# Attention's block border rewritten: projections, the whole weight sum and ScalarE's end-of-block work moved to one place, one addition for four heads

## The chip, the cores and the metric

The kernel runs on one core of one Trainium2 chip. The metric is the device time of one execution in microseconds; several runs of the same program are summarised by their median. A profiled execution gives, for every instruction, its start, its length and what it waited for. Four engines matter here: TensorE (PE, matmuls; its weight loads are listed as PEld), VectorE (DVE), ScalarE (ACT) and SyncE (SP, which issues transfers). Each takes its instructions strictly in the order of the program; between engines there are only semaphores.

## What is computed

The input is x of shape (16, 384, 16, 16) in float32. Four layers follow each other; only the first is touched by the change in what it computes with, the others by their order.

```python
def layer0(x, qk_w, alpha, beta, gamma):          # 2 batches x 2048 tokens, 12 heads of 32
    xt = tokens(x)                                # (2, 2048, 384)
    q, k = split(xt @ qk_w.T)                     # per head
    attn = softmax(q * 32**-0.5 @ k.T)            # (2, 12, 2048, 2048)
    attn = alpha * eye + beta * attn - gamma / 2048
    return attn @ xt_heads                        # v is x itself
```

Layer 1 is a ConvNeXt block (depthwise 7x7 convolution, layer norm, 384 to 1536, gelu, global response norm, 1536 to 384, residual), layer 2 a fusion block with depthwise 3x3 filters, a 768 to 384 matmul, norm and gelu, and layer 3 a linear-attention block with an MLP (384 to 1536 to 384). All of it is float32.

## The kernel before, in words

**Attention.** The function attention (L400) works through 6 units, one for each batch and group of four heads (128 channels). A unit has 4 blocks of 512 queries (NBLK), so there are 24 blocks, numbered 0 to 23. A block has 16 iterations (NQC), t = 0 to 15, one for each 128 keys. An iteration has these steps.

- scores (L465): four matmuls, one for each head, write st, two PSUM tiles of two heads each. Two ScalarE activations (exponential) turn them into e, 128 x 1024 each. Below, e(t) is the result of iteration t.
- weighted (L483): four matmuls add e times v into av. It is called one iteration late: PE gets st(t+1), then av(t).
- In weighted, too, VectorE adds e(t) to a running sum s, with two additions of 128 x 1024, one for each pair of heads. The tuple ADDS says after how many iterations a running sum is handed on: 16, 8 or 4 for each block.
- weights (L526): matmuls with a matrix of ones sum s over the keys and add it to dn, the softmax's denominator. In mid-block it is cut into four parts that are spread over later iterations; at the end of a block it is whole, four matmuls of 512 columns, two iterations after the block's last av.
- finish (L538) turns dn into a reciprocal and applies it: on ScalarE r (copy of dn), w (logarithm), w (exponential of the negative); on VectorE two refining steps r, then va times r, then the sum with xg. The steps are put one by one into the iterations 2 to 8 of the next block. va (copy of av) and xg are made by ScalarE right after the block's last av.
- project (L578): at iteration SLOT = 5 of a block, two steps of the projections: six matmuls p (three for each 128 x 512 result) and two ScalarE copies, into q of this unit or k of the next one. A step for k also issues the load of v on SP. Blocks 0 to 20 have two steps, block 21 has one, blocks 22 and 23 have none.

Three PSUM tiles of two banks (tag st) are shared by the scores and the projections; av and dn have a bank each. The e tiles last for four iterations.

**Order.** Everything goes through a recording layer (class InOrder, L98) which pins the instructions to the order in which the code emits them; that is why nearly all rows of the profile have the line L98. Work that is due later is kept in the dictionary due, by iteration. After each iteration, fill (L1505) puts work of layer 1 into VectorE's queue: mostly the depthwise 7x7 convolution (rows y<-l,vec,y; 48 multiply-add steps for each of 3 chunks of each of 8 blocks), and the first layer norms of two blocks. How much fits is reckoned by pace (L196) from assumed lengths: pe, the length of an iteration, less dve, VectorE's additions and finishing steps.

**Later work.** After attention a planner (class Plan, all at L182) orders the remaining tasks of layers 1 to 3 by assumed lengths, ranks (RANK) and a tolerance (SLACK).

Of the kernel before, what the change touches and what calls it, by code (L numbers as in the profile page):

```python
# [9 lines left out]
F32 = mybir.dt.float32  # L10
AF = mybir.ActivationFunctionType
ALU = mybir.AluOpType
# [3 lines left out]
P = 128  # L16
# [12 lines left out]
NBLK = N // BLK  # L29
NIP = NBLK  # L30
NQC = N // P
SLOT = 5
LEAD = 20 * NQC + 6
FIRST = NQC + 10

TURNS = (
    (0, ((0, 0), (0, 1), (0, 2), (0, 3),)),
# [6 lines left out]
AFTER = ('x4', 0, 2)  # L44

RANK = {
    "mid": ((7.3, 48.9, 70.4, 82.6), (148.1, 31.6, -5.4, 26.9)),
    "l1": ((125.5, 116.9, 31.6, 62.9), (92.4, 221.3, 38.4, 14.0)),
    "l3c": ((153.2, 335.5, -64.8, 29.8), (10.7, 30.4, 62.7, 79.9)),
    "conv": 470.9,  # L50
}
SLACK = 0.1944
LOGEXP = "natural_log_exp_and_others"
JUNK = 2

ADDS = (16, 16, 16, 16, 8, 16, 8, 4, 4, 16, 16, 16, 8, 8, 4, 8, 16, 16, 8, 8, 4, 8, 4, 4)
XB, YB, SB = 12, 4, 23
NLEAD = 2
TB = BLK // P
RB = 2 * HW  # L60
HD3 = 48
MOST, LEAST, TINY = 1e18, 1e-11, 1e-19
# [133 lines left out]
def pace(t):  # L196


    n, i = divmod(t - 1, NQC)
    adds = ADDS[n]  # L200
    pe, dve = 2.066, 2.275 if t and i % adds else 0.0
    at = i - adds - 1
    parts = sum(j * adds // 4 == at % adds for j in range(4)) if at >= 0 else 0
    if parts:
        pe += 0.22 * parts
    elif i == 1 and n > 0:
        pe += 0.87
    else:
        pe += 0.09
    if n > 0:  # L210
        dve += {5: 0.66, 6: 0.66, 7: 0.6, 8: 0.66}.get(i, 0.0)
    return pe, dve


# [185 lines left out]
def attention(tc, X, xt, L0, block, small, col, cols, ones, load_qk, banks, fill, bound, tiny):  # L400
# [6 lines left out]
    with ExitStack() as actx:  # L407
        pool = lambda name, bufs, **kw: actx.enter_context(tc.tile_pool(name=name, bufs=bufs, **kw))
        wqk_sb = pool("wqp", 1).tile([P, NC, 2, NC, P], F32, name="wqk_sb")
        load_qk(wqk_sb)  # L410
        ep = pool("ep", 8)
        sp = pool("sp", 4)
        op = pool("op", 2)
        pst = pool("pst", 3, space=PSUM)
        pacc = pool("pacc", 1, space=PSUM)
# [37 lines left out]
            return made, early, late  # L453


        due = {}

        def unit(u, made, gm):

            b, g = units[u]  # L460
            q, keys, v = made["q"], made["k"], made["v"]
            adds = ADDS[u * NBLK : (u + 1) * NBLK]
            acc, sums = {}, {}

            def scores(n, t):  # L465
                es = []
                for i in range(2):
                    es.append(ep.tile([P, 2, BLK], F32, tag="e", name=f"e_{u}_{n}_{t}_{i}"))
                sts = [bank2(f"st_{u}_{n}_{t}_{i}") for i in range(2)]
                for h in range(4):  # L470
                    rows = slice(HD * h, HD * (h + 1))
                    pe.matmul(
                        sts[h // 2][:, h % 2, :],
                        keys[t // TB][rows, ts(t % TB, P)],
                        q[n][rows, :],
                        start=True,
                        stop=True,
                    )
                for i in range(2):
                    act.activation(es[i], sts[i], AF.Exp, scale=HD**-0.5)  # L480
                return es

            def weighted(n, t, es):  # L483
                if t == 0:
                    acc["av"] = pacc.tile([P, BLK], F32, tag="av", name=f"av_{u}_{n}")
                for h in range(4):
                    pe.matmul(
                        acc["av"][HD * h : HD * (h + 1), :],
                        v[t // TB][:, (t % TB) * P + HD * h : (t % TB) * P + HD * (h + 1)],
                        es[h // 2][:, h % 2, :],  # L490
                        start=(t == 0),
                        stop=(t == NQC - 1),
                    )
                at = t % adds[n]
                for i in range(2):
                    if at == 0:
                        sums[i] = es[i]
                    elif at == 1:
                        s = sp.tile([P, 2, BLK], F32, tag="s", name=f"s_{u}_{n}_{t}_{i}")
                        dve.tensor_tensor(s, sums[i], es[i], ALU.add)  # L500
                        sums[i] = s
                    else:
                        dve.tensor_tensor(sums[i], sums[i], es[i], ALU.add)


                k = (u * NBLK + n) * NQC + t
                if at == adds[n] - 1:
                    parts = 1 if t == NQC - 1 else 4
                    for i in range(parts):
                        due.setdefault(k + 2 + i * adds[n] // 4, []).append(  # L510
                            lambda i=i, summed=dict(sums): weights(
                                n, t, summed, ts(i, BLK // parts)
                            )
                        )
                for f in due.pop(k, ()):
                    f()
                if t == NQC - 1:
                    va = op.tile([P, BLK], F32, tag="va", name=f"va_{u}_{n}")
                    act.activation(va, acc["av"], AF.Copy, scale=1.0)
                    xg = op.tile([P, BLK], F32, tag="xg", name=f"xg_{u}_{n}")  # L520
                    act.activation(
                        xg, X[b][n][:, g, :], AF.Identity, scale=col("alpha", g), bias=gm
                    )
                    due[k + 2].append(lambda: finish(n, va, xg))

            def weights(n, t, summed, at):  # L526
                if t == adds[n] - 1 and at.start == 0:
                    acc["dn"] = pacc.tile([P, BLK], F32, tag="dn", name=f"dn_{u}_{n}")
                for h in range(4):
                    pe.matmul(  # L530
                        acc["dn"][HD * h : HD * (h + 1), at],
                        ones[:, :HD],
                        summed[h // 2][:, h % 2, at],
                        start=(t == adds[n] - 1 and at.start == 0),
                        stop=(t == NQC - 1),
                    )

            def finish(n, va, xg):  # L538

                if g == 0:  # L540
                    L0[b][n] = block(f"l0_{b}_{n}")
                k = u * NBLK + n
                r = op.tile([P, BLK], F32, tag="r", name=f"r_{u}_{n}", bufs=1)
                w = op.tile([P, BLK], F32, tag="w", name=f"w_{u}_{n}", bufs=1)
                act.activation(r, acc["dn"], AF.Identity, accum_out=bound[:, 0, k : k + 1])

                def log():
                    act.activation(w, r, AF.Ln, bias=tiny)

                def invert():  # L550
# [12 lines left out]

                def put():
                    dve.scalar_tensor_tensor(
                        L0[b][n][:, g, :], va, col("beta", g), xg, ALU.mult, ALU.add
                    )

                for i, f in enumerate([log, invert, defect, refine, scale, put]):
                    due.setdefault((k + 1) * NQC + 3 + i, []).append(f)  # L570

            return scores, weighted

        means = [channel_means(dve, op, X, cols, b, act if b else None) for b in range(NB)]
        for b, (_, steps) in enumerate(means):
            for i, s in enumerate(steps):
                due[b * NC * NBLK * NQC - 36 * b + (3 - b) * i] = [s]
        def project(name, steps):  # L578
            pp = bank2(name)
            for copy in [f(pp[:, i, :]) for i, f in enumerate(steps)]:  # L580
                copy()
            return 2.7 * len(steps)

        made, early, late_steps = projections(*units[0])
        for i in range(0, len(early), 2):
# [4 lines left out]
        for u, (b, g) in enumerate(units):  # L590
# [5 lines left out]
            for n in range(NBLK):  # L596
                for t in range(NQC):
                    es = scores(n, t)
                    added = 0.0
                    if before:  # L600
                        before()
                    before = lambda f=weighted, a=(n, t, es): f(*a)
                    if t == SLOT and steps:
                        added = project(f"p_{u}_{n}", steps[:2])
                        del steps[:2]
                    fill((u * NBLK + n) * NQC + t, added)
            assert not steps
        before()
        while due:
            for f in due.pop(min(due)):  # L610
                f()
# [4 lines left out]
def conv_seq_kernel(  # L616
# [882 lines left out]
    if fast:  # L1499
# [5 lines left out]
        def fill(t, added=0.0):  # L1505
# [7 lines left out]
            if t % NQC == 10 and t > NQC:  # L1513
# [164 lines left out]
```

## Time and profile before

| what | value |
|---|---|
| median of 3 runs | 2658.92 us (2658.7 to 2660.63) |
| the profiled execution | 2660.87 us, of which the span from first to last instruction is 2659.1 |
| granted TensorE clock, mean | 0.996 |
| attention: first st to last av's start | 19.3 to 1027.7 us |
| additions s | 668 of 128 x 1024, mean 1.22 us |
| convolution y<-l,vec,y | 1152, 654.7 us busy |
| dn matmuls | 67.4 us busy; their weight loads waited 10.9 us for s |
| block's end on ScalarE, mean | va 0.60, xg 0.82, r 0.60 + 0.20, w 0.73, w 0.65 + 0.22 us |

A row of a group reads: line, engine, operation, out<-in, shapes, count, then busy time in us and the mean of one in ns, then how long the engine sat idle before it and for whom. A row of the timeline reads: start, length from the first start to the last end, engine, line, operation, out<-in, shapes, count, and in brackets the idle time ahead of it. Matmuls overlap, so the step from start to start is the cost of a matmul, not its length. A float32 matmul of the code is two instructions in the trace: the 4 matmuls of st(t) are a row of x8, six matmuls p are x12.

### The profile page before, as it was taken

The page shows a single profiled execution, that of the slowest core. Times are in us where ns is not written, and L with a number is a line of the kernel's source. Part 1 is how long each engine was busy: PE and PEld are TensorE (multiplying, and loading weights), DVE is VectorE, ACT ScalarE, POOL GpSimd, SP SyncE. Part 2 cuts the span into 40 slices and gives each one's busy share as a digit, 9 for nine tenths or more (in the row PEclk, how much of TensorE's full clock was granted, in tenths as well). Part 3 has the DMA queues.
Part 4 walks back from the last instruction along what each step waited for, and adds up shares of the span by engine and source line. Part 5 has one row for each costly group of instructions (what it writes and reads, how often), then busy time and mean ns, then how long its engine had stood idle before and what let it go on. Part 6 is the DMA issues. An engine that isn't in the chain of part 4 may idle for free. (4 is left out here: it accounts for less than half of the span.)

```text
span 2659.1 us, 30865 instructions
## 1 busy us (share of the span) xinstructions
PE 2623.8 (99%) x12005; PEld 1035.7 (39%) x12005; DVE 2028.8 (76%) x2604; ACT 1573.3 (59%) x2339; POOL 7.5 (0%) x54
## 2 busy tenths in 40 slices
PE   9999999999999999899999999999999999999999
PEld 2222232223222323344444544444444444445443
DVE  5999999999999989999999999999462140542300
ACT  6888888988888887454636534455246551415311
POOL 0000000000000000000000000000000000000000
PEclk9999999999999999899999999999999999999999
DMA  4000000000000003000001101101210000000000
GB/s 155 1 13 5 5 11 3 13 5 5 9 1 1 13 1 131 0 0 1 0 1 36 36 0 48 37 11 48 71 36 12 24 24 12 13 12 1 0 21 16
DMA packets 29275, 55.56 MB, mean 21 GB/s; under 512 B 1728, under 2 KB 14400, under 8 KB 29120
## 3 DMA queue, kind: packets, MB, share of 16 engines
q1 hardware_dynamic: 29120, 53.51, 6.0%
q8 instruction: 96, 1.57, 0.2%
q14 instruction: 59, 0.48, 0.1%
HBM read 47.21 MB, written 6.29 MB: 20 GB/s over the span
## 5 line engine op out<-in xcount | busy, mean ns | idle before, releaser
L98 ACT ACTIVATE e<-st 128x1024 f32<-128x1024 f32 x768 | 742.1, 1025 | 77.2 <-PE st L98 64.0
L98 DVE TENSOR_TENSOR s<-s,e 128x1024 f32<-128x1024 f32 x568 | 657.5, 1219 | 18.3 <-ACT e L98 17.4
L98 DVE SCALAR_TENSOR_TENSOR y<-l,vec,y 128x420 f32<-128x420 f32 (+8 forms) x1152 | 654.7, 636 | 3.6 <-ACT y L98 0.7
L98 PE MATMUL st<-q,k 32*128 32x512 f32 x3072 | 481.7, 641 | 2.9 <-ACT e L98 1.5
L98 PE MATMUL av<-e,v 128*32 128x512 f32 x3072 | 410.6, 605 | 6.1 <-ACT va L98 3.7
L98 PE MATMUL po_l<-hid_l,wb 128*128 128x512 f32 x576 | 259.7, 600 | 4.0 <-ACT hid_l L98 4.0
L98 PE MATMUL ph_l3c<-d_l3c,wa 128*128 128x512 f32 x576 | 259.1, 594 | 0.0
L98 PE MATMUL ph_l<-y,wa 128*128 128x512 f32 x576 | 258.6, 594 | 0.0
L98 PEld LDWEIGHTS st<-q,k 32*128 32x128 f32 x3072 | 152.0, 183 | 270.6 <-issue 145.7
L98 PE MATMUL po_l3c<-hid_l3c,wb 128*128 128x512 f32 x576 | 253.7, 593 | 0.0
L98 ACT ACTIVATE hid_l3c<-ph_l3c,vec 128x512 f32<-128x512 f32 x96 | 65.8, 687 | 264.8 <-PE ph_l3c L98 264.2
L98 PEld LDWEIGHTS av<-e,v 128*32 128x32 f32 x3072 | 60.6, 108 | 299.9 <-issue 273.0
L98 DVE SCALAR_TENSOR_TENSOR o_l3c<-po_l3c,vec,l 128x512 f32<-128x512 f32 x24 | 17.8, 749 | 197.7 <-PE po_l3c L98 196.6
L98 PEld LDWEIGHTS po_l<-hid_l,wb 128*128 128x128 f32 x576 | 109.4, 192 | 139.7 <-issue 127.6
L98 PEld LDWEIGHTS po_l3c<-hid_l3c,wb 128*128 128x128 f32 x576 | 109.0, 190 | 137.2 <-issue 136.2
L98 PEld LDWEIGHTS ph_l3c<-d_l3c,wa 128*128 128x128 f32 x576 | 108.7, 190 | 137.0 <-issue 130.7
L98 PEld LDWEIGHTS ph_l<-y,wa 128*128 128x128 f32 x576 | 108.5, 190 | 136.2 <-issue 126.1
L98 ACT ACTIVATE hid_l<-ph_l,vec 128x512 f32<-128x512 f32 x96 | 65.8, 686 | 135.1 <-PE ph_l L98 134.8
L98 DVE TENSOR_TENSOR s<-e,e 128x1024 f32<-128x1024 f32 x100 | 117.8, 1220 | 30.7 <-ACT e L98 26.1
L98 PE MATMUL p<-x,wqk_sb 128*128 128x512 f32 x288 | 131.8, 608 | 4.1 <-DMA x<-in_x_dram 4.1
L98 DVE SCALAR_TENSOR_TENSOR g_l3a<-h_l3a,dw,g_l3a 128x450 f32<-128x450 f32 (+1 forms) x192 | 119.2, 699 | 14.9 <-ACT g_l3a L98 14.7
L98 ACT ACT_TABLE_LOAD x88 | 112.9, 1283 | 16.7 <-PE ph_l L98 9.4
(153 smaller groups left out, 2285.8 us busy)
## 6 DMA issues: line engine op xcount, KB each, us to landing
wa<-in_w_dram SPq DMA_DIRECT2D x9, 768.0 KB, 4.3
wb<-in_w_dram SPq DMA_DIRECT2D x9, 768.0 KB, 4.8
wa<-in_mlp_w_dram SPq DMA_DIRECT2D x9, 768.0 KB, 4.3
wb<-in_mlp_w_dram SPq DMA_DIRECT2D x9, 768.0 KB, 4.4
v<-in_xt_dram SPq DMA_DIRECT2D x24, 256.0 KB, 2.7
out_dram<-o_l3c SPq DMA_DIRECT2D x24, 256.0 KB, 2.0
x<-in_x_dram SPq DMA_DIRECT2D x7, 768.0 KB, 11.0
qkv<-in_qkv_wT_dram SPq DMA_DIRECT2D x3, 576.0 KB, 11.5
```

What stands on the lines that cost most here:

```text
L98: self.last = self.tc.keep_in_program_order(make(*args, **kw))
```

## The change

- **Addition.** e is one tile of 128 x 2048 for four heads, still written by two activations. VectorE makes one addition of 128 x 2048 in place of two of 128 x 1024, all into the one running sum s. The pools have half as many tiles of twice the size.
- **Border.** SLOT is gone. At t = 0 of the next block, after st(0) and the last av of the block, the order is: va and xg on ScalarE; the first projection step; the whole weight sum dn on PE and r, w, w on ScalarE; the second projection step. VectorE's four finishing steps follow in iterations 1 to 4 of that block.
- **Parts.** Parts of a mid-block weight sum that would reach past the block's end are put at its iteration 15.
- **ADDS.** Six entries differ: 8 to 16 at blocks 6, 12, 18 and 21, 16 to 8 at blocks 11 and 16. Blocks with two groups go from eight to six.
- **pace** assumes 2.156 us for an iteration and ADD = 2.21 us for an addition; fill marks a block as done at iteration 6 in place of 10.
- **Later work.** RANK and SLACK have new values. In the built order VectorE's queue has 248 convolution steps before the last addition, where it had 212.

```diff
-ADDS = (16, 16, 16, 16, 8, 16, 8, 4, 4, 16, 16, 16, 8, 8, 4, 8, 16, 16, 8, 8, 4, 8, 4, 4)
+ADDS = (16, 16, 16, 16, 8, 16, 16, 4, 4, 16, 16, 8, 16, 8, 4, 8, 8, 16, 16, 8, 4, 16, 4, 4)
...
-    pe, dve = 2.066, 2.275 if t and i % adds else 0.0
+    pe, dve = 2.156, ADD if t and i % adds else 0.0
...
-                for i in range(2):
-                    if at == 0:
-                        sums[i] = es[i]
-                    elif at == 1:
-                        s = sp.tile([P, 2, BLK], F32, tag="s", name=f"s_{u}_{n}_{t}_{i}")
-                        dve.tensor_tensor(s, sums[i], es[i], ALU.add)
-                        sums[i] = s
-                    else:
-                        dve.tensor_tensor(sums[i], sums[i], es[i], ALU.add)
+                if at == 0:
+                    acc["s"] = es
+                elif at == 1:
+                    s = sp.tile([P, 4, BLK], F32, tag="s", name=f"s_{u}_{n}_{t}")
+                    dve.tensor_tensor(s, acc["s"], es, ALU.add)
+                    acc["s"] = s
+                else:
+                    dve.tensor_tensor(acc["s"], acc["s"], es, ALU.add)
...
+                if t == NQC - 1:
+                    ends.append(finish(n, acc["s"]))
...
+                def copies():
+                    act.activation(va, acc["av"], AF.Copy, scale=1.0)
...
+                def sum_up():
+                    weights(n, NQC - 1, summed, ts(0, BLK))
...
-                for i, f in enumerate([log, invert, defect, refine, scale, put]):
-                    due.setdefault((k + 1) * NQC + 3 + i, []).append(f)
+                for i, f in enumerate([defect, refine, scale, put]):
+                    due.setdefault((k + 1) * NQC + 1 + i, []).append(f)
+                return copies, sum_up, invert
...
+        def project(name, steps, between=()):
...
+            for i, f in enumerate(steps):
+                f(pp[:, i, :])()
+                if i == 0:
+                    for f in between:
+                        f()
...
-                    if t == SLOT and steps:
-                        added = project(f"p_{u}_{n}", steps[:2])
+                    if t == 0:
+                        between = ()
+                        if ends:
+                            copies, *between = ends.pop()
+                            copies()
+                        added = project(f"p_{u}_{n}", steps[:2], between)
```

More of the change, by code (lines that the diff above doesn't have):

```diff
@@ L31 @@
 NQC = N // P
-SLOT = 5
 LEAD = 20 * NQC + 6
-FIRST = NQC + 10
+FIRST = NQC + 6
 TURNS = (
@@ L46 @@
 RANK = {
[L47 to L50, printed above, removed]
+    "mid": ((46.7, 76.5, 79.7, 90.5), (32.4, -7.3, 105.9, 36.5)),
+    "l1": ((84.2, 93.7, 99.2, 30.9), (33.3, 89.9, 48.4, 85.5)),
+    "l3c": ((70.8, 9.1, 23.4, 134.4), (88.7, 61.2, 57.5, 98.1)),
+    "conv": 160.3,
 }
-SLACK = 0.1944
+SLACK = 0.1932
 LOGEXP = "natural_log_exp_and_others"
 JUNK = 2
-ADDS = (16, 16, 16, 16, 8, 16, 8, 4, 4, 16, 16, 16, 8, 8, 4, 8, 16, 16, 8, 8, 4, 8, 4, 4)
+ADDS = (16, 16, 16, 16, 8, 16, 16, 4, 4, 16, 16, 8, 16, 8, 4, 8, 8, 16, 16, 8, 4, 16, 4, 4)
 XB, YB, SB = 12, 4, 23
@@ L59 @@
 TB = BLK // P
+ADD = 2.21
 RB = 2 * HW
@@ L200, in pace @@
     adds = ADDS[n]
-    pe, dve = 2.066, 2.275 if t and i % adds else 0.0
+    pe, dve = 2.156, ADD if t and i % adds else 0.0
     at = i - adds - 1
[L203 to L207, printed above, removed]
-    else:
-        pe += 0.09
+    if at >= 0:
+        pe += 0.22 * sum(j * adds // 4 == at % adds for j in range(4))
+        pe += 0.22 * (adds < 8 and i == NQC - 1)
     if n > 0:
-        dve += {5: 0.66, 6: 0.66, 7: 0.6, 8: 0.66}.get(i, 0.0)
+        dve += {1: 0.66, 2: 0.66, 3: 0.6, 4: 0.66}.get(i, 0.0)
     return pe, dve
@@ L410, in attention @@
         load_qk(wqk_sb)
-        ep = pool("ep", 8)
-        sp = pool("sp", 4)
+        ep = pool("ep", 4)
+        sp = pool("sp", 2)
         op = pool("op", 2)
@@ L453, in projections @@
             return made, early, late
-        due = {}
+        due, ends = {}, []
         def unit(u, made, gm):
@@ L462, in unit @@
             adds = ADDS[u * NBLK : (u + 1) * NBLK]
-            acc, sums = {}, {}
+            acc = {}
             def scores(n, t):
-                es = []
-                for i in range(2):
-                    es.append(ep.tile([P, 2, BLK], F32, tag="e", name=f"e_{u}_{n}_{t}_{i}"))
+                es = ep.tile([P, 4, BLK], F32, tag="e", name=f"e_{u}_{n}_{t}")
                 sts = [bank2(f"st_{u}_{n}_{t}_{i}") for i in range(2)]
@@ L479, in scores @@
                 for i in range(2):
-                    act.activation(es[i], sts[i], AF.Exp, scale=HD**-0.5)
+                    act.activation(es[:, 2 * i : 2 * i + 2, :], sts[i], AF.Exp, scale=HD**-0.5)
                 return es
@@ L489, in weighted @@
                         v[t // TB][:, (t % TB) * P + HD * h : (t % TB) * P + HD * (h + 1)],
-                        es[h // 2][:, h % 2, :],
+                        es[:, h, :],
                         start=(t == 0),
@@ L494, in weighted @@
                 at = t % adds[n]
-                for i in range(2):
-                    if at == 0:
-                        sums[i] = es[i]
-                    elif at == 1:
-                        s = sp.tile([P, 2, BLK], F32, tag="s", name=f"s_{u}_{n}_{t}_{i}")
-                        dve.tensor_tensor(s, sums[i], es[i], ALU.add)
-                        sums[i] = s
-                    else:
-                        dve.tensor_tensor(sums[i], sums[i], es[i], ALU.add)
-                k = (u * NBLK + n) * NQC + t
[L507 to L513, printed above, removed]
+                if at == 0:
[6 more added lines that the diff above has]
+                    dve.tensor_tensor(acc["s"], acc["s"], es, ALU.add)
+                k = (u * NBLK + n) * NQC + t
+                if t == NQC - 1:
+                    ends.append(finish(n, acc["s"]))
+                elif at == adds[n] - 1:
+                    for i in range(4):
+                        due.setdefault(min(k + 2 + i * adds[n] // 4, k - t + NQC - 1), []).append(
+                            lambda i=i, summed=acc["s"]: weights(n, t, summed, ts(i, P))
                         )
@@ L516, in weighted @@
                     f()
[L517 to L524, printed above, removed]
             def weights(n, t, summed, at):
@@ L532, in weights @@
                         ones[:, :HD],
-                        summed[h // 2][:, h % 2, at],
+                        summed[:, h, at],
                         start=(t == adds[n] - 1 and at.start == 0),
@@ L536, in weights, with finish, invert @@
                     )
-            def finish(n, va, xg):
-                if g == 0:
-                    L0[b][n] = block(f"l0_{b}_{n}")
+            def finish(n, summed):
                 k = u * NBLK + n
+                va = op.tile([P, BLK], F32, tag="va", name=f"va_{u}_{n}")
+                xg = op.tile([P, BLK], F32, tag="xg", name=f"xg_{u}_{n}")
                 r = op.tile([P, BLK], F32, tag="r", name=f"r_{u}_{n}", bufs=1)
                 w = op.tile([P, BLK], F32, tag="w", name=f"w_{u}_{n}", bufs=1)
-                act.activation(r, acc["dn"], AF.Identity, accum_out=bound[:, 0, k : k + 1])
-                def log():
+                def copies():
+                    act.activation(va, acc["av"], AF.Copy, scale=1.0)
+                    act.activation(
+                        xg, X[b][n][:, g, :], AF.Identity, scale=col("alpha", g), bias=gm
+                    )
+                def sum_up():
+                    weights(n, NQC - 1, summed, ts(0, BLK))
+                def invert():
+                    act.activation(
+                        r, acc["dn"], AF.Identity, accum_out=bound[:, 0, k : k + 1]
+                    )
                     act.activation(w, r, AF.Ln, bias=tiny)
-                def invert():
                     act.activation(
@@ L564, in put @@
                 def put():
+                    if g == 0:
+                        L0[b][n] = block(f"l0_{b}_{n}")
                     dve.scalar_tensor_tensor(
@@ L577, in attention @@
                 due[b * NC * NBLK * NQC - 36 * b + (3 - b) * i] = [s]
[L578 to L582, printed above, removed]
+        def project(name, steps, between=()):
+            pp = bank2(name) if steps else None
+            for i, f in enumerate(steps):
[3 more added lines that the diff above has]
+                        f()
+            if not steps:
+                for f in between:
+                    f()
+            return 2.7 * len(steps) + (0.88 if between else 0.0)
         made, early, late_steps = projections(*units[0])
@@ L608, in attention @@
         before()
+        for f in ends.pop():
+            f()
         while due:
@@ L1512, in fill @@
                 return
-            if t % NQC == 10 and t > NQC:
+            if t % NQC == 6 and t > NQC:
                 u, i = divmod(t // NQC - 1, NBLK)
```

## The prediction

> **What bounds the kernel now.** I read the page's busy shares first, then the timeline around one block's border, then the groups of additions, then the granted clock in short windows.
>
> ```profile
> PE 2623.8 (99%) x12005; PEld 1035.7 (39%) x12005; DVE 2028.8 (76%) x2604; ACT 1573.3 (59%) x2339; POOL 7.5 (0%) x54
> ```
> and from the sums by stretch (columns: length, then busy time of PE, weight load, VectorE, ScalarE, GpSimd, then granted clock, DMA share, GB/s)
> ```profile
> 300.00:500.00 200.00, 198.93 (x1531) 60.35 (x1528) 192.99 (x204) 171.95 (x220) 0.00 (x0) 1.00 0.03 8
> ```
> PE is busy 99%, but in attention (19.3 to 1028.3 us) VectorE is at 96% too (192.99 of 200): whichever is delayed decides. The border of block 3 in the timeline:
> ```profile
> 139.65 11.44 DVE L98 TENSOR_TENSOR s<-s,e 128x1024 f32<-128x1024 f32 x10
> ...
> 146.79 1.06 PE L98 MATMUL av<-e,v 128*32 128x512 f32 x8
> 146.89 1.94 ACT L98 ACTIVATE e<-st 128x1024 f32<-128x1024 f32 x2 [0.29 <-PE st L98]
> ...
> 148.72 0.60 ACT L98 ACTIVATE va<-av 128x512 f32<-128x512 f32 x1
> ...
> 152.92 1.04 PE L98 MATMUL dn<-s,ones 128*32 128x512 f32 x8
> ...
> 153.90 1.14 PE L98 MATMUL st<-q,k 32*128 32x512 f32 x8
> ...
> 160.27 5.42 PE L98 MATMUL p<-x,wqk_sb 128*128 128x512 f32 x12
> ...
> 165.61 1.14 PE L98 MATMUL st<-q,k 32*128 32x512 f32 x8
> ...
> 190.14 0.60 ACT L98 ACTIVATE va<-av 128x512 f32<-128x512 f32 x1
> ```
> From va to va a block of one weight sum takes 41.42. The st rows step by 2.07 and 2.24 in turn, 2.155 on average (141.41, 143.49, 145.72). The dn costs 153.90 - 152.92 = 0.98, both projections 165.61 - 160.27 = 5.34. So 16 x 2.155 + 0.97 + 5.34 = 40.8: only 0.6 to 0.8 is lost to ScalarE's block-end work. The last addition ends at 151.09 (the last of the x10 begins at 149.86), dn runs 1.8 later: VectorE is late, but nobody waits.
>
> Now the price of a joined addition. From the groups (after the bar: busy us, mean ns of one, idle before):
> ```profile
> L98 DVE TENSOR_TENSOR s<-s,e 128x1024 f32<-128x1024 f32 x568 | 657.5, 1219 | 18.3 <-ACT e L98 17.4
> ...
> L98 DVE TENSOR_TENSOR y<-y,s_l 128x1536 f32<-128x1536 f32 x8 | 14.0, 1756 | 0.2
> ```
> and from VectorE's timeline, a pair that waits as the joined additions will:
> ```profile
> 1096.30 1.49 DVE L98 TENSOR_TENSOR s_l<-s_l,s_l 128x512 f32<-128x512 f32 x2
> ```
> An addition of 1024 lasts 1.219, of 1536 1.756; by that slope 2048 lasts 2.286. The x10 row gives (11.44 - 1.22) / 9 = 1.135 from start to start: neighbours are of different tiles, and overlap by 0.083. The s_l pair is one of two links of a chain, with a wait for VectorE itself and one for ScalarE, just as the joined additions have: 1.49 = 2 x 0.693 + 0.104. There is no overlap, but a bubble of 0.104.
>
> **The change part by part.**
>
> *One addition for four heads.* In the changed order ten of a block's fifteen additions wait for the one directly ahead: 2.286 + 0.104 = 2.390 each, where the pair took 2 x 1.135 = 2.270. Four have a finishing step between (2.203), the last counts whole (2.286). The Trainium skill (VectorE: DVE Perf Modes, The TRN2 errata) speaks for the change: a fixed latency per instruction is paid once by one large tile; and The DRAIN you can't avoid says that semaphores cost nothing extra. By that a pair of 2 x 1.22 becomes 2.29, 0.15 saved, 2.3 a block. By the rows it is 10 x 0.12 lost and some 5 x 0.07 saved, 0.9 lost. I take the rows: the same kind of wait is in the s_l row. With four finishing steps (0.68 to 0.75 less 0.083, together 2.47), the chain from the first addition's start to the last one's end is 10 x 2.390 + 4 x 2.203 + 2.286 + 2.47 = 37.5.
>
> *Weight sum and ScalarE at the border.* The new PE order is st(0), av(15), three matmuls of the projections, dn, three matmuls, st(1). PE makes the fifteenth e 14 x 2.155 = 30.2 after e(1), and asks for dn 1.2 + 2.67 later (rest of av, half of 5.34), at 34.0. VectorE is done at 37.5 + 0.1. So dn stalls 3.7 us, where two whole iterations covered it before. Behind dn in PE's queue stand the second projection, st(1), and so ScalarE's e(1) and the next block's first addition. From the last addition: 0.1 + 0.98 + 2.67, then 3.11 from st to its second e's end (165.61 to 168.73), 0.06: 6.9. The convolution steps put there (7 to 9, 4.3 to 5) hide in it. Period 37.5 + 6.9 = 44.4, against 41.42. Were VectorE in time it would be 40.7. ScalarE's steps cost nothing: va and xg lie under the first projection, r (0.79), logarithm (0.72) and exponential (0.87) under the second with 0.2 to spare. Beyond that they'd cost their excess each border, at most 1 us; I take 0. The projections' loads of v, on SP's queue, go out five iterations earlier and are needed a unit later; the DMA share there is 0.03, so nothing waits. The e tiles still last four iterations: e(t+4) waits for addition t. The twelfth ends at 30.4, when e(16) would start anyway: 0, and where VectorE starts late the loss lies inside dn's stall.
>
> *ADDS.* Two blocks fewer with two groups: 0.88 of PE each, but two more additions. Blocks of 8: chain 35.0, but 12 to 14 convolution steps (7.2 to 8.4) exceed the 6.9, and VectorE never rests: about 42.8 (before 41.96). Blocks of 4: 43.4 (before 42.8 to 42.95).
>
> *Sum of attention.* Block 0's chain holds three channel sums: border at 47.5. Then ten of 44.4, five of 42.8, three of 43.4: 836 from block 1's first st to block 20's; the timeline has 798 (62.59 to 860.46): +38. The first projection now fills the start, where av waits for its load: -4.7. Blocks 20 to 23: the last two borders lack one or both projections, dn asks earlier and stalls up to 8, r to the exponential lie open: +8. Together +42.
>
> *The clock.* Does a stall of 3.7 slow PE?
> ```profile
> 21.56:24.97 3.41, 1.45 (x8) 0.41 (x12) 1.64 (x2) 2.65 (x3) 0.00 (x0) 1.00 1.02 402
> 24.97:28.38 3.41, 3.41 (x20) 0.72 (x16) 0.72 (x1) 0.10 (x1) 0.00 (x0) 0.50 0.81 312
> ...
> 960.20:967.10 6.90, 5.21 (x40) 1.54 (x40) 4.99 (x3) 6.86 (x9) 0.00 (x0) 1.00 0.00 0
> ```
> A window of 3.41 with 1.96 idle was followed by one at half clock; 0.85 idle in each of two windows was not. The Trainium skill (TensorE: Matmul & The Clock Gate, What's actually happening) lets the clock fall after a wholly idle window of about 3.4 us. By that a stall of 3.7 would almost never count: +2 us in all. By the rows a stall of 3.7 leaves at least 1.85 idle in one window, next to the 1.96 that did count. Half clock for one or two windows, partly within the stall, loses 1.3 to 2.9 on dn, projection and st(1), all on the path. With some 12 such borders: 0 to +35; I take +20, nearer to the row.
>
> *Later work.* From 1028.3 to 2652.5 PE has 15.3 idle in 1624, 10.1 of it at 1063 to 1074 where pg and po wait behind convolutions. The new order has VectorE's matching point 36.4 after the last addition (37.2 before): the wait stays. It adds a wait for sv ahead of po (some 5), and 36 convolution steps (20 us of VectorE) are already done. VectorE has slack after 1900, so that shortens nothing by itself. Bounds -10 to +8; I take +2.
>
> Sum: span 2659.1 + 42 + 20 + 2 = 2723. The profiled execution took 2660.87 and the median of the runs is 2658.92, 0.2 under the span: 2723 for the time, too.
>
> **The rivals.**
> A, faster: VectorE keeps up, and the cover at the border pays. Its point is an addition of (34.0 - 2.5) / 15 = 2.10 or less. Then borders run at 40.7 and, with the start, 20 us go: 2639. Against it: 2048 elements already take 2.13 by the slope, and the free spacing is 2.20.
> B, the bubble is smaller. Single-wait links (the convolution's chain) show 0.035: chain 36.8, stall 3.0, attention +28, 2689 without clock loss. No bubble at all: chain 35.5, stall 1.8, attention +7, 2668. For it: no row of before has 2048 elements.
> C, the later order repays more: all of the 15 idle is gone, 2705 or, without clock loss, 2686. Against: po's new wait.
>
> **How the numbers follow.** A measurement tells 0.2% (5 us) from no change. Forecast 0.72 (2700 to 2745), A 0.06, B 0.17 (of which 0.04 within 0.2%), C 0.05. Faster 0.06, same 0.04, slower 0.90. Predicted 2723. The range, 2680 to 2745, leaves out A, the lower half of B and 0.05 above: 0.19.
>
> **What would show it.** dn's wait for s should be the largest wait of PE, 50 to 75 us (10.9 now); joined additions 2.286 with 0.104 idle between; va to va 44 to 47 in blocks of 16; granted clock below 1 in attention; attention's last av near 1070 to 1092. If dn waits under 20 us, the chain is wrong; if it waits but the clock stays at 1.00, the 20 us are wrong.

## The result, and the profile after

| | before | after |
|---|---|---|
| median, same chip | 2658.88 us | 2729.11 us (2727.19 to 2731.85) |
| ratio | | 1.0263, interval 1.0246 to 1.0281 |
| span of the profiled execution | 2659.1 us | 2727.4 us |
| mean granted TensorE clock | 0.996 | 0.987 |

The changed kernel is 70 us slower; 2723 was forecast. I cut the two spans at four marks that every version has: the first st of blocks 1 and 20, and attention's last av.

| stretch | before | after | difference | forecast |
|---|---|---|---|---|
| up to block 1's first st | 62.6 | 66.9 | +4.3 | -4.7 |
| blocks 1 to 19 | 797.9 | 853.2 | +55.3 | +38, and most of the clock's 20 |
| block 20's first st to the last av | 167.2 | 179.4 | +12.2 | +8 |
| last av to the end | 1631.4 | 1628.0 | -3.4 | +2 |

The busy shares on the page of after, to be held against 99 and 76 before:

```profile
PE 2653.5 (97%) x11941; PEld 1037.5 (38%) x11941; DVE 2022.3 (74%) x2272; ACT 1581.8 (58%) x2336; POOL 7.4 (0%) x54
```

TensorE's busy time grew by 30 although it has 64 instructions fewer: part of it ran at half clock. The same stretch as before, 300 to 500, and blocks 1 to 19 (length, busy time of TensorE, weight load, VectorE, ScalarE, GpSimd, then clock):

```profile
300.00:500.00 200.00, 189.47 (x1377) 56.32 (x1378) 180.16 (x139) 154.83 (x188) 0.00 (x0) 0.96 0.02 6
...
66.87:920.03 853.16, 816.47 (x5721) 233.57 (x5717) 784.39 (x562) 684.18 (x810) 0.00 (x0) 0.98 0.02 6
```

TensorE and VectorE, both nearly full before (198.93 and 192.99), now both have 10 to 20 us of 200 idle. That fits two engines that wait for each other in turn, and not one that has too much work. The timeline of the border behind block 2, in order of time:

```profile
128.86 2.29 DVE L98 TENSOR_TENSOR s<-e,e 128x2048 f32<-128x2048 f32 x1 [1.97 <-ACT e L98]
...
140.15 26.24 DVE L98 TENSOR_TENSOR s<-s,e 128x2048 f32<-128x2048 f32 x11
...
160.22 2.84 PE L98 MATMUL p<-x,wqk_sb 128*128 128x512 f32 x6
...
166.31 4.68 DVE L98 SCALAR_TENSOR_TENSOR y<-l,vec,y 128x392 f32<-128x392 f32 x7
...
166.44 1.93 PE L98 MATMUL dn<-s,ones 128*32 128x512 f32 x8 [3.38 <-DVE s L98]
...
168.31 5.05 PE L98 MATMUL p<-x,wqk_sb 128*128 128x512 f32 x6
...
173.29 1.14 PE L98 MATMUL st<-q,k 32*128 32x512 f32 x8
...
176.44 2.29 DVE L98 TENSOR_TENSOR s<-e,e 128x2048 f32<-128x2048 f32 x1 [5.45 <-ACT e L98]
```

The row of x11 gives the step of a joined addition behind another: (26.24 - 2.29) / 10 = 2.395. VectorE's chain runs from 128.86 to 140.15 + 26.24 = 166.39, 37.5 us. TensorE has done the first projection at 163.06 and stands for 3.38 until the sum is there. Then dn takes 1.93 and the second projection 5.05, where the first one took 2.84 and dn takes 1.07 at full clock (in x5b below): half clock. Only behind them come st(1), its e, and, 10 us after the last addition, VectorE's next one. The group and the waits of TensorE and of its weight load (waited in all, times, longest):

```profile
L98 DVE TENSOR_TENSOR s<-s,e 128x2048 f32<-128x2048 f32 x288 | 659.3, 2289 | 23.5 <-ACT e L98 1.6
```

```profile
PEld dn L98 <- DVE s L98: 65.5, 27, 7.0
...
PE dn L98 <- DVE s L98: 44.2, 18, 6.0
...
PE p L98 <- ACT k L98: 2.9, 2, 2.3
```

The wait of dn's weight loads for s went from 10.9 to 65.5; its matmuls, which had no such wait before, now have 44.2. The stalls lie at the twelve borders behind a block of 16 in ADDS: 1.4 to 3.7 up to block 19, and 6.0 ahead of block 22, whose border has no projection as cover. Behind blocks of 8 or 4, which make one or three additions fewer, the border's dn waits for nothing up to block 21. What more blocks of 8 would have saved was not tried.

### The profile page after: what moved, and what is told of

The parts are those of the page before. It is cut to its first block, busy times and chain, and to the rows that moved or that the text cites. A ratio compares the mean times of both kernels' runs of the same rounds, so it can differ in the third digit from the quotient of the medians.

```text
span 2727.4 us, 29765 instructions
## 1 busy us (share of the span) xinstructions
PE 2653.5 (97%) x11941; PEld 1037.5 (38%) x11941; DVE 2022.3 (74%) x2272; ACT 1581.8 (58%) x2336; POOL 7.4 (0%) x54
## 5 line engine op out<-in xcount | busy, mean ns | idle before, releaser
L98 DVE TENSOR_TENSOR s<-s,e 128x2048 f32<-128x2048 f32 x288 | 659.3, 2289 | 23.5 <-ACT e L98 1.6
L98 DVE TENSOR_TENSOR s<-e,e 128x2048 f32<-128x2048 f32 x48 | 109.8, 2287 | 78.2 <-ACT e L98 75.5
L98 PE MATMUL p<-x,wqk_sb 128*128 128x512 f32 x288 | 154.2, 678 | 7.6 <-DMA x<-in_x_dram 3.9
L98 ACT ACTIVATE hid_l<-hid_l,vec,gx_l 128x256 f32<-128x256 f32 x192 | 103.1, 615 | 19.0 <-DVE gx_l L98 19.0
## 6 DMA issues: line engine op xcount, KB each, us to landing
x<-in_x_dram SPq DMA_DIRECT2D x7, 768.0 KB, 10.9
qkv<-in_qkv_wT_dram SPq DMA_DIRECT2D x3, 576.0 KB, 10.9
```

The source lines that it names most:

```text
L98: self.last = self.tc.keep_in_program_order(make(*args, **kw))
```

## The experiments

The theory: dn, put earlier in TensorE's order, waits for a chain of additions that the joined tile made longer and coarser, and the stall lowers the clock. Rivals: the joined addition is slow by itself; the position alone costs; the later order costs. Each kernel was timed with runs of the kernel before on its chip; ratios are to these.

| kernel | median, us | ratio, interval | blocks 1 to 19 | last av to end |
|---|---|---|---|---|
| after | 2729.11 | 1.0263 (1.0246 to 1.0281) | 853.2 | 1628.0 |
| x1_two_tiles | 2676.54 | 1.0066 (1.0049 to 1.0083) | 814.0 | 1625.4 |
| x2_sum_later | 2719.62 | 1.0223 (1.0206 to 1.0240) | 813.1 | 1664.2 |
| x3_both_first | 2706.92 | 1.0175 (1.0158 to 1.0192) | 831.5 | 1627.8 |
| x4_before_joined | 2663.37 | 1.0012 (1.0005 to 1.0019) | 800.0 | 1631.5 |
| x5_warm | 2722.31 | 1.0233 (1.0216 to 1.0250) | 848.2 | 1627.9 |
| x6_finish_border | 2745.98 | 1.0317 (1.0299 to 1.0334) | 838.3 | 1657.2 |
| x8_sum_after_st1 | 2740.56 | 1.0303 (1.0286 to 1.0320) | 821.4 | 1675.4 |
| x10_split_ends | 2705.91 | 1.0174 (1.0157 to 1.0191) | 833.0 | 1626.6 |
| x5b_warm_two | 2712.16 | 1.0200 (1.0185 to 1.0216) | 836.5 | 1627.9 |
| x8b_sum_after_st1_same_plan | 2678.35 | 1.0074 (1.0058 to 1.0089) | 808.6 | 1627.2 |
| x9_two_tiles_start | 2674.86 | 1.0061 (1.0046 to 1.0077) | 814.3 | 1625.4 |
| x7b_two_tiles_start_finish | 2673.18 | 1.0053 (1.0039 to 1.0067) | 812.0 | 1626.9 |

### One part alone, or undone

**x1_two_tiles**: the changed kernel with two additions of 1024 again.

```
-                es = ep.tile([P, 4, BLK], F32, tag="e", name=f"e_{u}_{n}_{t}")
+                es = [ep.tile([P, 2, BLK], F32, tag="e", name=f"e_{u}_{n}_{t}_{i}") for i in range(2)]
...
-                    dve.tensor_tensor(acc["s"], acc["s"], es, ALU.add)
+                    for i in range(2):
+                        dve.tensor_tensor(acc["s"][i], acc["s"][i], es[i], ALU.add)
```

> Edit: the changed kernel with its additions split again into two of 128x1024 into two running sums; border, ADDS, later order and the convolution steps placed (ADD still 2.21) as changed. Theory T (VectorE's chain of a block is too long for the new dn, and the stall also halves the granted clock): the pair takes 2.27 in place of 2.39, so the chain of a 16-block goes from 37.5 to 36.6 and dn's stall from 3.4 to about 2.6. That is 10 us by length alone, and 5 to 20 more if stalls of 2.6 leave the clock alone more often: 2700 to 2719. Rival R1 (the joined addition with its bubble is the whole loss): back to 2655 to 2670. Rival R2 (the additions don't matter, the place of the sum alone does): 2724 to 2734.

**x4_before_joined**: the kernel before with the joined addition, and nothing else.

```
-                for i in range(2):
-                    if at == 0:
-                        sums[i] = es[i]
...
+                if at == 0:
+                    acc["s"] = es
...
+                    dve.tensor_tensor(acc["s"], acc["s"], es, ALU.add)
```

> Edit: the kernel before with the joined addition of 128x2048 alone; its border, ADDS, convolution placement and later order unchanged. Theory T: an addition behind another one costs 2.39 against 2.27 for the pair, one behind something else 2.20: about +0.9 us of VectorE in a 16-block that has 0.8 idle, no dn stall: 0 to +0.8 a block, 2660 to 2676. Rival S (one large instruction pays the fixed cost once, waits cost nothing: 2.29 against 2 x 1.22): VectorE gains 2.3 a block, PE bounds anyway: 2655 to 2659.

x1 gives back 53 of the 70 us; x4 loses 3. So the joined addition costs little where dn stands late, and most of the loss where dn stands at the border. My theory had x1 too slow (2700 to 2719), and rival R1 had it too fast (2655 to 2670). The border of x1 behind block 3 shows why:

```profile
200.04 2.19 PE L98 MATMUL dn<-s,ones 128*32 128x512 f32 x8 [0.43 <-DVE s L98]
201.04 4.89 DVE L98 SCALAR_TENSOR_TENSOR y<-l,vec,y 128x420 f32<-128x420 f32 x7
...
202.16 2.84 PE L98 MATMUL p<-x,wqk_sb 128*128 128x512 f32 x6
...
207.16 2.36 DVE L98 TENSOR_TENSOR s<-e,e 128x1024 f32<-128x1024 f32 x2 [1.23 <-ACT e L98]
```

With two tiles dn's first two heads start while VectorE still adds the other two (dn lasts 2.19 and not 1.06), and the next block's first addition needs half of e(1) only. So the two tiles save at both ends of the chain, beside a shorter chain. TensorE is held 0.43 ahead of dn and 1.1 more within it, 1.5 in all and not 3.38, and the clock stays at 1.00 over blocks 2 to 19. I had counted the chain alone.

**x10_split_ends** takes those two ends alone: the first and last addition of a block in halves, those between joined.

```
+                    parts = 2 if t in (1, NQC - 1) else 1
+                    for i in range(parts):
+                        h = ts(i, 4 // parts)
+                        dve.tensor_tensor(s[:, h, :], acc["s"][:, h, :], es[:, h, :], ALU.add)
```

> The changed kernel with the first and the last addition of a block in two halves of 1024 (on the same tiles), all between them joined. Unit theory: what the joined addition costs at the border is that it waits for both halves of e(1) (0.97 us later than the first half) and that dn waits for all four heads (half of dn could lie beside the second half: 0.5); two halves at the ends give back 1.0 to 1.5 us at some 19 borders and part of the clock: 2690 to 2710, near the version with all additions split (2676.5). Rival, the bubble of 0.104 behind each of the ten joined additions in the middle is what counts: 2715 to 2730, since these are kept.

2705.9 lies in the theory's interval. Over blocks 1 to 19 it saves 20.2 of the 39.2 us that x1 saves, so the unit of waiting at the ends accounts for about half of the joined tile's price there. But both figures hold the clock's share. Against x5b below, which keeps the joined additions and holds the clock (836.5), x1 saves 22.5 and x10 3.5; x10 still has two half-clock windows of 3.4 there, which cost it at most 1.7 each (an estimate: half their length). So split ends shorten the borders by 3.5 to 7 us in all, and most of the 20.2 is the clock kept. How the rest divides between the 0.12 of each addition in the middle and those two windows wasn't separated.

### The place of dn

**x3_both_first**: both projections ahead of dn.

```
             for i, f in enumerate(steps):
                 f(pp[:, i, :])()
-                if i == 0:
-                    for f in between:
-                        f()
+            for f in between:
+                f()
```

> Edit: the changed kernel with both projection steps ahead of dn, and r, logarithm and exponential behind it, uncovered. Theory T: PE asks for s 2.67 later, so the stall falls from 3.4 to under 1 and no half clock follows (about 27 us back); ScalarE's uncovered steps cost less than the second projection did behind dn: period of a 16-block about 43. 2680 to 2700. Rival R3 (ScalarE's steps need the projection's cover, each border loses their 2.4 us): 2735 to 2750 less what the clock gives back, so 2715 or more.

Blocks 1 to 19 fell by 21.7, the whole by 22. At the borders up to block 21 dn's matmuls no longer wait for s, and from block 2 to 19 the clock stays at 1.00. x3 missed its interval by 7 us, and the trace shows two new waits at each border. The second projection's matmuls wait 0.68 for the first one's copy. And e(1) starts 2.24 after st(1), where it is 1.17 in after: r, the logarithm and the exponential now stand ahead of it on ScalarE. So rival R3 holds in part: ScalarE's steps do need the projection's cover, for about 1.1 of their 2.4 us.

**x2_sum_later** put dn, r, the logarithm, the exponential and the finishing steps back into later iterations, where the kernel before has them, with the budget of fill set to match:

```
-                return copies, sum_up, invert
+                due.setdefault((k + 1) * NQC + 1, []).append(later)
+                for i, f in enumerate([log, invert, defect, refine, scale, put]):
+                    due.setdefault((k + 1) * NQC + 3 + i, []).append(f)
+                return (copies,)
```

**x8_sum_after_st1** moved only dn and ScalarE's three, behind st(1) and av(0):

```
-                return copies, sum_up, invert
+                due.setdefault((k + 1) * NQC, []).extend([sum_up, invert])
+                return (copies,)
```

> Edit: the changed kernel with dn and ScalarE's r, logarithm and exponential back two to four iterations into the next block, VectorE's finishing steps in iterations 5 to 8 as before; joined additions, projections, va and xg at the border stay. Theory T: dn finds s ready, PE's waits for s fall from 66 us to under 15, the clock stays at 1.00 in attention but for the start; VectorE's whole work (42 us a 16-block) becomes the bound, so 2672 +- 10. Rival R1 (the joined addition is the loss): stays above 2710. Rival R2 (projections at t = 0 or the later order are the loss): stays above 2700 with the waits for s gone.

> The changed kernel with only the block's last weight sum (dn) and ScalarE's r, logarithm and exponential moved: behind the next block's st(1) and av(0), so that both projections, st(1) and av(0) lie ahead of dn on TensorE. Finishing steps, convolution steps per iteration and the order of later work as in the changed kernel. Position theory: dn then asks 4.9 us later than now and finds its sum ready, no stall, clock 1.00, and the later part stays as in the changed kernel (1622 us from the last av of attention on, which the earlier version with dn in the next block's iterations did not keep, since its number of convolution steps per block was another): 2672 to 2692. Rival, the later part's loss of some 30 us in that earlier version came with dn's position itself: 2705 to 2720. Rival, the joined additions are slow by themselves and VectorE sets the period: blocks of 16 stay at 44 or more, 2710 to 2730.

Both missed, but not by attention: there they saved 40 and 32 us (blocks 1 to 19). They lost 36 and 47 behind it. The waits of TensorE in x8 from 1061 to 1410, in which after has nothing above 3.6:

```profile
PE sv_l L98 <- DVE s_l L98: 9.0, 3, 4.5
PE pg_l L98 <- DVE gs_l L98: 6.6, 1, 6.6
PE pf_l L98 <- DVE ex_l L98: 6.2, 1, 6.2
PE po_l L98 <- ACT hid_l L98: 5.5, 2, 3.5
```

The cause was a slip of mine in both: project adds 0.88 us to fill's budget only if dn lies between the projections. Without it fewer convolution steps went into attention, and the later order did not fit; for x8 the next run shows this, for x2 it is inferred. Steps ahead of the last addition in VectorE's queue, counted as in the 248 and 212 above, and the time behind attention:

| | order of before, 212 steps | changed order, 248 (after) | 233 (x6) | 213 (x8) | 199 (x2) |
|---|---|---|---|---|---|
| last av to end, us | 1631.4 | 1628.0 | 1657.2 | 1675.4 | 1664.2 |

**x8b_sum_after_st1_same_plan** is x8 with the 0.88 restored (248 steps) and the projections' copies behind both matmul groups.

```
                         added = project(f"p_{u}_{n}", steps[:2], between)
+                        added += 0.88 if u or n else 0.0
```

> As x8_sum_after_st1, with two slips of it mended: the fill gets its 0.88 us per block back, so that attention takes in the same 248 convolution steps as in the changed kernel (x8 had 213, and its later part, ordered for 248, grew from 1622 to 1675 us); and both projections' matmuls lie ahead of both copies (the second waited 0.7 for the first one's copy). Position theory with VectorE as the bound: x8's attention ended at 1061; the 35 steps that come back are 23 us of VectorE, which is busy nearly all the time, so it ends at 1072 to 1084, and the later part takes 1622 to 1626: 2695 to 2709, some 20 to 30 below the changed kernel. If TensorE sets the time instead, attention ends at 1048 to 1060: 2672 to 2684. Rival, the later part's loss was not due to the number of steps: over 2725.

2678.35: the later part is back at 1627.2, and the place of dn and of ScalarE's three, with the copies out of the way, is worth 51 us. Of the two cases it was TensorE's: VectorE's lack of slack, which I had taken for the bound, did not show. The border behind block 2 of x8b, to be held against that of after:

```profile
140.01 19.06 DVE L98 TENSOR_TENSOR s<-s,e 128x2048 f32<-128x2048 f32 x8
...
153.09 5.42 PE L98 MATMUL p<-x,wqk_sb 128*128 128x512 f32 x12
...
158.43 1.14 PE L98 MATMUL st<-q,k 32*128 32x512 f32 x8
...
158.99 4.68 DVE L98 SCALAR_TENSOR_TENSOR y<-l,vec,y 128x392 f32<-128x392 f32 x7
...
160.39 1.04 PE L98 MATMUL dn<-s,ones 128*32 128x512 f32 x8
```

The same joined additions, the same step, (19.06 - 2.29) / 7 = 2.396; the last ends at 159.07, and dn, at 160.39, waits for nothing. Either remedy alone, x1 or x8b, takes 51 to 53 of the 70 us away: that loss belongs to the pair.

### The clock

**x5_warm** keeps TensorE busy in the stall with four matmuls whose results are thrown away, **x5b_warm_two** with two.

```
                 if i == 0:
+                    if warm is not None and len(steps) == 2:
+                        for _ in range(2):
+                            pe.matmul(pp[:, 1, :], ones, warm[:, 0, :], start=True, stop=True)
                     for f in between:
                         f()
```

> The changed kernel with four more matmuls of 128x512 (about 0.44 us each, 1.8 in all; their results are thrown away) on TensorE between the first projection and dn, at the twelve borders behind a block of 16 additions. They lie where TensorE stands waiting for the last addition, so they take no time from the chain of additions; only the idle stretch is broken up. Clock theory: the changed kernel runs 55 us of attention at half clock, which loses about 27 us of TensorE's work on the path. No 3.4 us window is left with 1.9 us idle behind these borders, so most half-clock stretches go: 2702 to 2714 us, and the granted clock of the attention back at 1.00. Rival, the stall alone costs and what runs at half clock is hidden in later slack: 2725 to 2733. Second rival, the clock falls in spite of these matmuls (because the wait, not the idle share of a window, does it): half-clock stretches stay, 2728 to 2745.

> As x5_warm with two extra matmuls in place of four. In x5_warm the clock stayed at 1.00 from 16 to 955 us, but four took 3.70 us and not 1.8 (a matmul of these lasts 0.92: the profile's row for a projection's three counts six), so dn began 1.06 us after its sum was there, and at every border. Two (1.85) and the 0.68 ahead of them fit into the stall. The gap from st(0) to st(1) should be 13.15 - 1.06 = 12.1 at the eleven stalled borders of blocks 1 to 19, where the changed kernel has 13.62 on average (14 to 15.3 with half clock, 10.1 to 11.1 without). Clock theory: 11 x 1.5 = 17 us back: 2706 to 2716, with the clock at 1.00 in attention up to block 20. Rival, half clock costs nothing of its own, since dn's end is set by VectorE: 2722 to 2730. Rival, without the extra matmuls the clock falls after windows with about 1.95 us idle, and two are too few: half-clock stretches come back, 2716 to 2730.

x5 kept the clock up to 955 us, but its dose was wrong: a float32 matmul is two instructions, so four took 3.7 us and held dn up. x5b came out inside its interval. Its border behind block 2, and blocks 1 to 19:

```profile
161.69 1.98 PE L98 MATMUL p<-x,ones 128*128 128x512 f32 x4 [0.68 <-ACT k L98]
164.26 4.68 DVE L98 SCALAR_TENSOR_TENSOR y<-l,vec,y 128x392 f32<-128x392 f32 x7
164.40 1.07 PE L98 MATMUL dn<-s,ones 128*32 128x512 f32 x8 [0.73 <-DVE s L98]
165.39 2.84 PE L98 MATMUL p<-x,wqk_sb 128*128 128x512 f32 x6
```

```profile
66.22:902.76 836.54, 819.81 (x5764) 235.57 (x5760) 784.48 (x562) 683.96 (x810) 0.00 (x0) 1.00 0.02 6
```

The chain is as long as in after and dn still waits for it, but dn and the projection last 1.07 and 2.84, not 1.93 and 5.05. 853.2 - 836.5 = 16.7 us of the stretch were the clock's, and the whole is 17 us faster for doing more work.

### What else was tried for a faster version

**x6_finish_border** put VectorE's four finishing steps ahead of the next block's first addition, to shorten the chain:

```
-                for i, f in enumerate([defect, refine, scale, put]):
-                    due.setdefault((k + 1) * NQC + 1 + i, []).append(f)
+                for f in [defect, refine, scale, put]:
+                    due.setdefault((k + 1) * NQC, []).append(f)
```

> The changed kernel with the four finishing steps of VectorE put at the border too, ahead of the next block's first addition, in place of one each behind the additions 1 to 4 of the next block. Chain theory (the prediction's): fourteen joined additions at 2.390 and one of 2.286 make 35.75 instead of 37.5, so dn's stall behind a block of 16 shrinks by 1.8 us at twelve borders (about 3 to about 1.3), and the four steps (2.5 us) fit into the 5 to 6 us in which VectorE has nothing but convolution steps there: 21 us back, and with the half-clock stretches mostly gone 10 to 25 more: 2682 to 2705. Rival, dn's stall comes from the joined tile as the unit of waiting and not from the length of the chain: 2715 to 2730. Rival, the steps delay the next block's first addition (they wait for the exponential): 2725 to 2745.

Blocks 1 to 19 fell by 15, but my change to the step budget left 233 steps in attention, and the later part rose by 29. **x9_two_tiles_start** is x1 with both matmul groups of the early projections ahead of both copies, as before; **x7b_two_tiles_start_finish** adds x6's edit with 248 steps kept.

```
+            if not between:
+                for copy in [f(pp[:, i, :]) for i, f in enumerate(steps)]:
+                    copy()
+                return 2.7 * len(steps)
```

> The version with all additions split in two tiles (x1, 2676.5), and the projections ahead of attention issued as in the kernel before, both matmul groups ahead of both copies. Start theory: the changed kernel's and x1's first st came 3.6 to 5.6 us later than before's because each second step's matmuls wait for the first one's copy (0.7 and 2.3 us gaps on TensorE); that is on the path: 2670 to 2674. Rival, the time is only moved to the next wait (the loads of the first values): 2675 to 2679.

> As x9_two_tiles_start, with VectorE's four finishing steps at the border, ahead of the next block's first addition, and the number of convolution steps kept. Chain theory: in x1 dn stalls 0.5 to 2.1 us at eleven borders (16.7 us in all over blocks 1 to 19); a chain shorter by 2.5 us takes most of it: 10 to 16 us less than x9_two_tiles_start, 2656 to 2664, level with the kernel before (2659 to 2660). Rival, the gap ahead of the first addition is full of convolution steps already, so that finishing steps and convolution steps push the first addition back: in x6 borders into blocks behind 8 additions rose from 9.0 to 10.5 that way: no gain or a loss, 2668 to 2685.

x9's block 1 starts 3.3 us earlier than x1's, and the span is 3.0 shorter; the medians differ by 1.7, less than a measurement tells, so neither side is shown. x7b gains nothing that can be told either. Its borders show that the rival holds: behind block 3 its chain is shorter by the finishing steps, but the next block's first addition starts 4.3 us after st(1) (201.89 against 197.55), where x9 has 2.2, since finishing and convolution steps fill the gap.

No version beat the kernel before. x1, x8b, x9 and x7b all stay 14 to 19 us above it. In x8b these lie at the start (4.5), in blocks 1 to 19 (10.7) and in the last four blocks (6.9), less 4.2 behind attention. VectorE does 36 more convolution steps within attention than before there, some 23 us of work; whether these or ScalarE's steps in one row cost the 10.7 wasn't tried and stays open.

## Why the prediction was right

**The joined addition.** Forecast 2.286 long and 2.390 from one to the next; measured 2.289 and 2.395. The slope of the two rows that the prediction shows, 0.537 for 512 elements, gives 2.293 and not 2.286, and 2.15 and not 2.13 for the elements alone; over a chain that is 0.1 us. Rival A needed 2.10, rival B a smaller bubble than 0.104: it is 0.106. Both fall. The Trainium skill's statement that the semaphore costs nothing extra (VectorE: DVE Perf Modes, The DRAIN you can't avoid) was measured there on a chain of copies; read as a rule for these additions it would have given a gain. Measured alone, in x4, the joined addition is 3 us slower.

**The chain and the stall.** Chain 37.5, measured 37.5. dn asked at 34.0 behind the first addition, measured 163.06 - 128.86 = 34.2; stall 3.7, measured 3.4. From the last addition to the next block's first 6.9: at the border behind block 1, which ran at full clock, the additions end at 121.90 and start again at 128.86, 7.0. Period 44.4; x5b, which has the stall without the clock's loss, has 44.5 in block 3.

**Blocks 1 to 19 without the clock.** Forecast 836 us, and 836.5 in x5b. The agreement is partly luck: the ten borders behind 16 additions gave 45.1 on average (43.5 to 46.9) where 44.4 was forecast, those behind 8 additions gave 42.2 (42.8), those behind 4 gave 42.7 (43.4), and block 1 gave 46.0 (47.5).

**The clock.** Forecast 20; 16.7 in these blocks by x5b; two more stretches of half clock, from 961 and 1012 us on, lie in the last four blocks. The row of before that I took (half clock after 1.96 of a 3.41 us window idle) was the better guide than the idle window of the skill (TensorE: Matmul & The Clock Gate, What's actually happening), read as wholly idle, which would have given 2: none of the eight windows ahead of half clock in blocks 1 to 19 was wholly idle (1.95 to 3.12 of 3.41). The 20 stood for all of attention; what half clock cost in the last four blocks lies in their +12.2 and wasn't measured apart.

**The start: wrong.** "The first projection now fills the start: -4.7", it was +4.3: the first st came 5.6 later (24.9 against 19.3) and block 0 was 1.3 shorter. I had not read out of the diff that project now makes each step's copy before it begins the next step's matmuls. In front of attention that is a wait on TensorE: the two waits of p for k in the list above, 2.9 together. Undone in x9, it gives 3.3 against x1 (block 1's first st at 59.3 and 62.6). The joined addition has the other part: x1 is 4.2 ahead of after there, 2.2 of it in block 0 and 2.0 ahead of the first st, where after ran at half clock for 3.4 us from 12.4 us on and x1 did not. Whether that window is more than chance isn't shown. Before, too, ran at half clock for 3.4 us in its block 0 (from 25.0 us on), which took 43.3; x4, with the same border and no such window there, took 40.7. So the filled start, 38.8 in x9 with two tiles, is by that estimate worth nearer 2 than 4.7, and with the joined tile and the old order of copies it wasn't run.

**The last four blocks: too small.** +8, measured +12.2. The uncovered dn ahead of block 22 stalled 6.0 as foreseen (up to 8), but a half-clock stretch of 10.2 us from 1012.5 on came with it.

**Later work.** +2, measured -3.4, within the bounds of -10 to +8. The wait of 6.5 and 3.6 for pg and po became three of 3.6, 2.4 and 1.9 for su, pg and sv. So the new order, with 36 more steps done ahead of it, pays a little, far from what rival C asked.

The terms make 63.3 (64 with attention's rounded 42) and came to 68.3: start 9.0 too low, last blocks 4.2 too low, later work 5.4 and clock 3.3 too high, blocks 0.6 too low. That the sum misses by 5 only is in part luck: 13.8 of misses on one side stand against 8.7 on the other.

The prediction named the pair, joined addition and early dn, as one chain, and so had its size. It did not say how little either half costs alone; that is what x4 (3 us), x1 and x8b (16 to 19 us with all else of the change) add.

## What to carry to other kernels

Before a consumer is moved ahead in an engine's queue, reckon when it will ask and when its input is ready: here dn asked 5.2 us behind st(0) in after, where nothing held it, and 9.4 to 9.8 in x8b, behind the second projection, st(1) and av(0), and that was worth 51 us over the kernel. A merged instruction waits for its last input and holds back its first output; splitting only the first and last link of a chain gave 23 of the 70 us back, mostly because the clock stayed up. Where an order is worked out for one amount of earlier work, keep that amount when you change something else, or compare only the stretch ahead of it.

## What the chip showed that I had not expected

The clock falls after little idle time. Three windows of after, each with the next one:

```profile
73.81:77.22 3.41, 1.46 (x9) 0.46 (x10) 1.90 (x1) 0.33 (x1) 0.00 (x0) 1.00 0.00 0
77.22:80.63 3.41, 3.41 (x5) 1.35 (x4) 0.00 (x0) 1.80 (x5) 0.00 (x0) 0.50 0.02 5
118.18:121.59 3.41, 1.48 (x4) 0.38 (x2) 3.31 (x2) 1.29 (x3) 0.00 (x0) 1.00 0.00 0
121.59:125.00 3.41, 3.05 (x13) 1.21 (x14) 3.27 (x6) 1.85 (x4) 0.00 (x0) 1.00 0.02 5
...
957.86:961.27 3.41, 1.91 (x14) 0.59 (x16) 2.30 (x3) 1.50 (x2) 0.00 (x0) 1.00 0.00 0
961.27:964.68 3.41, 3.41 (x28) 0.93 (x20) 2.05 (x1) 0.66 (x2) 0.00 (x0) 0.50 0.00 0
```

Eight windows of attention in after, themselves at full clock, had 1.95 us or more of 3.41 idle, and half clock followed each. Below that it is mixed: 1.93 at 118 us and 1.70 at 70 us kept the clock, 1.91 at 1009 us and 1.50 at 958 us lost it, and in x3 0.68 (from 62.12 us on) did. The windows lie at fixed times: the half-clock stretches of after start at 77.2, 166.0, 213.8, 302.5, 350.3 and 486.8 us, which is 26, 14, 26, 14 and 40 times 3.413 apart. So it matters where a stall falls: x10 has four stalls of 2.5 to 2.6 up to block 19, and the clock fell behind two of them. What else decides, beside the idle time, the runs do not show. And matmuls that do nothing useful, put into a stall, made the kernel 17 us faster.
